# One place per odd step for VectorE jobs, and a second only beside a TensorE job

## The chip, the cores and the metric

The kernel runs on one core of a Trainium2 chip. The metric is device time in microseconds (us), from launch to end. The kernel before takes 6031.49 us in the median of three runs (6030.53 to 6031.90).

The engines are called as the profile calls them: PE is TensorE, DVE is VectorE, ACT is ScalarE, POOL is GpSimd, SP is SyncE, which here only issues DMAs. PEld is the weight load of PE.

## The reference

The input x has 4 images of 128 channels and 64 x 64 pixels, float32. Two layers follow each other:

```
layer 0   Q, K, V = x Wq + bq, x Wk + bk, x Wv + bv      4 heads of 32 channels, 4096 tokens per image
          y = softmax(Q K^T * 32^-0.5) V Wo + bo + x      then a layer norm over channels
layer 1   spatial  = 3x3 convolution of y
          spectral = irfft2( W [Re rfft2(y); Im rfft2(y)] )
          mamba    = in_proj -> causal conv of 4 taps -> silu -> x_proj -> dt = softplus(dt_proj)
                     h_t = exp(dt A) h_(t-1) + dt B_t x_t,   y_t = C_t h_t + D x_t
                     (256 inner channels, 16 states each, 4096 tokens in order)
                     -> times silu(z) -> out_proj
          output   = spatial + spectral + mamba
```

Everything is float32. The attention scores and the scan over 4096 tokens with 16 states are the bulk of the work.

## The kernel before

**Tiles and steps.** An image is cut into 8 chunks of 512 tokens, so there are 32 chunks (`CHUNKS`), and a chunk has two halves with two heads each (64 halves, `HALVES`). The main loop (line 1064) counts steps `t`. A half takes 32 steps, one per block of 128 keys; a chunk takes 64 steps (`SLOT`). Below, "period c" is steps 64c to 64c + 63, and "step s of a period" is t mod 64.

**What every step does, in the order of writing.** `scores_for_exp` (line 488): six matmuls, at line 496, write scores less the row maximum into a PSUM buffer `s2`, and ACT takes the exponential (line 504). `scores_for_max` (line 443): four matmuls, at line 456, write the scores of a half that comes later into a PSUM buffer `s1`, and DVE reduces them to maxima (line 463). There is one buffer `s1` and one `s2`: the next step's matmuls wait until DVE and ACT have read them. `times_values` (line 507): the exponentials of the step before are multiplied with V (line 516) into a buffer `o`; at the end of a half ACT and DVE copy it out (lines 526 and 527).

**The scan.** It runs 144 steps (`LAG`) behind its chunk's attention, one state of one half of the channels in two steps. An even step runs `scan_state` (line 836): a scan on DVE (846), then on POOL a copy of the last column (855), a multiplication with C (856) and a sum (875). An odd step runs `scan_decay` (823), an exponential on ACT (829) into one PSUM buffer, and `scan_input_term` (831), a multiplication on POOL (834) for the state that DVE scans three steps later. There are two buffers each for these terms (`db`) and for the states (`hs`).

**The jobs.** All else is written as jobs (generators). They are put on the list with `plan.at` (lines 1032 to 1059) for a step and with a rank. A job runs until its next `yield`, which says what it needs to go on: `"P"` a place on TensorE, `"D"` on VectorE, `"A"` on ScalarE, `"B"` a free one of two PSUM banks. `Plan.step` (line 125) goes through the jobs once in a step, by rank, then by time, and lets go on each one for which there are places. Places are given anew in each step (lines 1095 to 1106):

```
        elif odd:
            plan.step(t, {"D": 2, "P": 2, "A": 2})
        else:
            plan.step(t, {"D": 0, "P": 0, "A": 1})
```

After step 2048, when the attention is done, there are more places (line 1099), and before the first half too (line 1102).

**Jobs that the text speaks of**, by chunk, with the lines of their parts:
- `project_kv` (342), `project_q` (408): projections; a matmul, then ACT and DVE split the result in two (lines 356, 357 and 418, 419).
- `output_projection` (569): a matmul (575), a sum on DVE (578), four transposes (582), nine DVE instructions for mean and variance (589 to 595), small instructions on ACT and POOL, and the normalisation on DVE (612).
- `normalise` (531): DMAs and a multiplication on POOL (560).
- `mamba_input` (646): transposes (663), then it puts `scan_input` and `spectral` on the list.
- `scan_input` (685), once per half of the channels: a matmul (689), ACT (693 to 695), four taps on DVE with a place each (699, 704), a sigmoid (624; ACT 628, 630, 633, 638 and DVE 636), and a multiplication on POOL (714).
- `scan_bc` (720): two matmuls (726), ACT and DVE (731 to 733).
- `scan_dt` (740), once per half of the channels: a matmul (744), six steps on ACT (750 to 765), then with one place on DVE and ACT an addition on DVE (766) and three multiplications or subtractions on POOL (767 to 769), here called a burst; some steps later ACT scales a tile (776).
- `gate` (779): a matmul (785), ACT, a sigmoid, and a multiplication on POOL (793), for each half of the channels.
- `convolve` (919): ten matmuls (930, 935), then ACT (940).
- `scan_output` (963), `spectral` (889), `flips` (1009).

**Order on an engine.** Nothing reorders what is written: each engine takes its instructions in the order in which the program wrote them (`manual_schedule`, line 181), and waits where its operand or its buffer isn't ready. A job's turn in a step so sets its place in the queues of all engines that it uses, of SP too.

Of the kernel before, what the change touches and what calls it, by code (L numbers as in the profile page):

```python
# [17 lines left out]
P = 128  # L18
# [83 lines left out]
class Plan:  # L102
# [19 lines left out]
    def release(self, bank, steps=1):  # L122
        self.freed.append((self.t + steps, bank))

    def step(self, t, places):

        self.t = t
        self.places |= places
        self.free += [bank for when, bank in self.freed if when <= t]
        self.freed = [e for e in self.freed if e[0] > t]  # L130
        for e in sorted((e for e in self.later if e[0] <= t), key=lambda e: e[:3]):
            self.jobs.append((e[1], e[0], e[2], Job(e[3])))
            self.later.remove(e)
        self.jobs = sorted((j for j in self.jobs if not j[3].done), key=lambda j: j[:3])
        kept = 0
        for *_, job in self.jobs:
            bank = None
            if "B" in job.need and len(self.free) <= kept:
                continue
            if any(c != "B" and not self.places[c] for c in job.need):  # L140
                kept += "B" in job.need
                continue
            for c in job.need:
                if c == "B":
                    bank = self.free.pop(0)
                else:
                    self.places[c] -= 1
            job.advance(bank)

            while not job.done and job.need in ("PAD" if self.late else "P"):  # L150
                if not job.need or not self.places[job.need]:
                    break
                self.places[job.need] -= 1
                job.advance(None)
        self.jobs = [j for j in self.jobs if not j[3].done]
# [6 lines left out]
def attention_then_conv_mamba(  # L162
# [43 lines left out]
    for h in range(HEADS):  # L206
        k, j = divmod(h, 2)
        c = COL["bk"] + k
# [8 lines left out]
    for h in range(HEADS):  # L217
        k, j = divmod(h, 2)
        c = COL["bq"] + h
# [108 lines left out]
    plan = Plan(2, {"x": 2, "f": 1})  # L328
# [114 lines left out]
    def scores_for_max(H, s):  # L443


        k = H % PAIRS
        m, t = divmod(s, TPC)
        assert have["K", k, m] == H // PAIRS // NCH
        if s == 0:
            part[H] = att.tile([P, 2, TPC, NCH], F32, tag="part", name=f"part_{H}")  # L450

        tag = "s2" if H == 0 and s % 2 else "s1"
        sc = psum.tile([P, 2, L], F32, tag=tag, name=f"s1_{H}_{s}")
        for n in range(2):
            for j in range(2):
                nc.tensor.matmul(  # L456
                    sc[:, j, :],
                    QT[H][rows[j], n, t::TPC],
                    KK[k][m][rows[j], :],
                    start=n == 0,  # L460
                    stop=n == 1,
                )
        nc.vector.tensor_reduce(part[H][:, :, t, m], sc, AX.X, ALU.max)  # L463
# [24 lines left out]
    def scores_for_exp(H, m):  # L488

        k = H % PAIRS  # L490
        i, t = divmod(m, TPC)
        assert have["K", k, i] == H // PAIRS // NCH
        s = psum.tile([P, 2, L], F32, tag="s2", name=f"s2_{H}_{m}")
        for n, mov in enumerate((QT[H][:, 0, :], QT[H][:, 1, :], MX[H])):
            for j in range(2):
                nc.tensor.matmul(  # L496
                    s[:, j, :],
                    sel[rows[j], :] if n == 2 else KK[k][i][rows[j], t * P : (t + 1) * P],
                    mov[rows[j], :],
                    start=n == 0,  # L500
                    stop=n == 2,
                )
        e = att.tile([P, 2, L], F32, tag="e", name=f"e_{H}_{m}", bufs=3)
        nc.scalar.activation(e, s, AF.Exp)  # L504
        es[H, m] = e

    def times_values(H, m):

        k = H % PAIRS
        i, t = divmod(m, TPC)  # L510
        assert have["V", i] == H // PAIRS // NCH
        if m == 0:
            po[H] = psum.tile([P, L], F32, tag="o", name=f"po_{H}")
        e = es.pop((H, m))
        for j in range(2):
            nc.tensor.matmul(  # L516
                po[H][used[j], :],
                VA[i][:, t, 2 * k + j, :],
                e[:, j, :],
                start=m == 0,  # L520
                stop=m == NT - 1,
            )
        if m == NT - 1:
            p = po.pop(H)
            oz[H] = att.tile([P, L], F32, tag="oz", name=f"oz_{H}", bufs=1)
            nc.scalar.activation(oz[H][used[0], :], p[used[0], :], AF.Identity)
            nc.vector.tensor_copy(oz[H][used[1], :], p[used[1], :])  # L527
# [295 lines left out]
    def scan_decay(c, v):  # L823
        n, hf = divmod(v, NH)
        k = hf * NS + n

        tag = "o" if plan.t >= HALVES * NT + 2 and v % 2 else "dA"
        dA[c, v] = psum.tile([P, L], F32, tag=tag, name=f"dA_{c}_{k}")
        nc.scalar.activation(dA[c, v], dts[c][hf], AF.Exp, scale=negA[:, k : k + 1])  # L829
# [6 lines left out]
    def scan_state(c, v):  # L836

        n, hf = divmod(v, NH)
        k = hf * NS + n
        assert (c, hf) in scaled  # L840
        late = plan.t > HALVES * NT + 1
        if late:
            hs = flat(VA[v % 4])
        else:
            hs = loc.tile([P, L], F32, tag="hs", name=f"hs_{c}_{k}")
        nc.vector.tensor_tensor_scan(  # L846
            hs,
            dA.pop((c, v)),
            db.pop((c, v)),
            state[:, k : k + 1] if c % NCH else zero,  # L850
            ALU.mult,
            ALU.add,
        )
        if c % NCH < NCH - 1:
            nc.gpsimd.tensor_copy(state[:, k : k + 1], hs[:, L - 1 :])  # L855
        nc.gpsimd.tensor_tensor(hs, hs, bcs[c, n][1], ALU.mult)  # L856
        if hf == NH - 1 and (c, n) in taken:
            spare.append((plan.t + 6, taken.pop((c, n))))
        elif hf == NH - 1:
            ring[0] += 1  # L860
        if late:

            if c not in sums_late:
                sums_late[c] = psum.tile(
                    [P, NH, L], F32, tag=f"s{1 + c % 2}", name=f"acc_{c}"
                )
            terms = [hs] if n else [xss[c][hf], hs]
            for x in terms:
                waiting.append((plan.t + 4, c, hf, x, n == NS - 1 and x is hs))
        elif n == 0:  # L870
            acc = loc.tile([P, L], F32, tag=f"acc{hf}", name=f"acc_{c}_{hf}")
            accs[c, hf] = acc
            nc.gpsimd.tensor_tensor(acc, xss[c][hf], hs, ALU.add)
        else:
            nc.gpsimd.tensor_tensor(accs[c, hf], accs[c, hf], hs, ALU.add)  # L875
# [185 lines left out]
    t = 6 - SLOT  # L1061
    loaded = 0
    end = (CHUNKS + 3) * SLOT
    while t < end or not plan.idle():
        H, m = divmod(t, NT)
        if 0 <= H < HALVES:
            scores_for_exp(H, m)
        h1, s1 = divmod(t + LEAD, NT)
        if 0 <= h1 + 1 < HALVES:
            scores_for_max(h1 + 1, s1)  # L1070
        H, m = divmod(t - 1, NT)
        last = m == NT - 1
        if last and 0 <= H < HALVES:
            times_values(H, m)
        c, s = divmod(t - LAG, SLOT)
        odd = s % 2 == 1
        if -1 <= c < CHUNKS:
            v = c * STATES + s // 2
            if not odd:
                if v >= 0:  # L1080
                    scan_state(*divmod(v, STATES))
            else:
                if 0 <= v + 1 < CHUNKS * STATES:
                    scan_decay(*divmod(v + 1, STATES))
                if 0 <= v + 2 < CHUNKS * STATES:
                    late = t > HALVES * NT
                    scan_input_term(
                        *divmod(v + 2, STATES), nc.vector if late else nc.gpsimd
                    )

                if loaded < CHUNKS * NS and loaded // NS in bcds:
                    if ring[0] or spare and spare[0][0] <= t:
                        scan_load(*divmod(loaded, NS))
                        loaded += 1
        plan.late = t > HALVES * NT
        if plan.late:
            add_states()
            if odd:
                plan.step(t, {"D": 4, "P": 4, "A": 6})
            plan.t = t  # L1100
        elif t < -LEAD:
            plan.step(t, {"D": 4, "P": 4, "A": 4})
        elif odd:
            plan.step(t, {"D": 2, "P": 2, "A": 2})
        else:
            plan.step(t, {"D": 0, "P": 0, "A": 1})
        if not last and 0 <= H < HALVES:
            times_values(H, m)
        t += 1
# [76 lines left out]
```

## Time and profile before

| what | value |
|---|---|
| runs (median of three) | 6031.49 us |
| the profiled execution | 6027.62 us |
| its span, first to last instruction | 6025.8 us |
| mean granted TensorE clock | 0.988 |
| start of step 0 to start of step 2047 | 5676.7 us (128.6 to 5805.3), 2.773 us a step |
| PE busy | 97% of the span |
| POOL, DVE, ACT busy | 74%, 71%, 59% |
| reduction of a step's scores, DVE line 463 | 1221 ns, 2048 times |
| scan, DVE line 846 | 1275 ns |
| exponential of a step's scores, ACT line 504 | 1023 ns, 2048 times |
| exponential for the scan, ACT line 829 | 686 ns, 1024 times |
| term, state and sum, POOL lines 834, 856 and 875 | 1284, 1278 and 1281 ns |

Busy time says little here for PE, as its matmuls overlap and their ends are modelled. It is of more use to look at steps: the time from the first matmul of line 496 in one step to that of the next. A step with no job on PE takes 2.355 us. Rows of the timeline begin with the start and the length in us, then engine, line, operation, output <- inputs, sizes, how many, and in brackets the idle time of the engine just before and what ended it.

### The profile page before, as it was taken

What the parts mean: (1) busy time and instruction counts of PE and PEld (TensorE: products, weight loads), DVE (VectorE), ACT (ScalarE), POOL (GpSimd) and SP (SyncE); (2) the same over time, 40 slices, a digit from 0 to 9 for tenths busy, and PEclk for the clock granted to TensorE, in tenths of its full rate; (3) what the DMA queues carried; (4) which work ended last, traced back from release to release, by engine and by line L of the source; (5) the groups of instructions that cost most, each with busy time, mean ns of one, the idle gap of its engine ahead of it and who ended that gap; (6) DMA issues with size and microseconds to landing.
All of it is one profiled execution on the core that took longest, in us unless ns stands there. A gap on an engine that the chain in (4) does not pass through costs nothing. (4 is left out here: it accounts for less than half of the span.)

```text
span 6025.8 us, 82754 instructions
## 1 busy us (share of the span) xinstructions
PE 5844.9 (97%) x31126; PEld 2786.9 (46%) x31126; DVE 4307.5 (71%) x4505; ACT 3548.3 (59%) x4762; POOL 4486.9 (74%) x4523
## 2 busy tenths in 40 slices
PE   5999999999999999999999999999999999999976
PEld 3444444444444444444444444444444444444422
DVE  4557777777777777777777777777777777777657
ACT  1455666666666666666666666666666666656653
POOL 0006888778888777888787888877888888788887
PEclk7999999999999999999999999999999999999988
DMA  4012222223232222223433322322433222222232
GB/s 125 25 37 56 67 72 75 71 71 111 82 89 73 74 70 74 74 67 88 105 83 82 78 64 73 75 71 68 109 81 86 70 64 64 67 71 64 62 99 90
DMA packets 312722, 456.34 MB, mean 76 GB/s; under 512 B 92768, under 2 KB 94336, under 8 KB 312320
## 3 DMA queue, kind: packets, MB, share of 16 engines
q1 hardware_dynamic: 307664, 449.18, 27.8%
q8 instruction: 244, 4.00, 0.3%
q10 hardware_dynamic: 4656, 1.87, 0.1%
q14 instruction: 158, 1.29, 0.1%
HBM read 376.21 MB, written 66.32 MB: 73 GB/s over the span
## 5 line engine op out<-in xcount | busy, mean ns | idle before, releaser
L463 DVE TENSOR_REDUCE part<-s 128x2 f32<-128x1024 f32 x2048 | 2499.3, 1221 | 1455.6 <-PE s L456 1455.2
L504 ACT ACTIVATE e<-s 128x1024 f32<-128x1024 f32 x2048 | 2095.1, 1023 | 2188.2 <-PE s L496 2178.9
L516 PE MATMUL po<-e,V 128*33 128x512 f32 x8192 | 2180.9, 605 | 2.3 <-DVE oz L527 0.3
L496 PE MATMUL s<-Q,K 64*128 64x512 f32 x8192 | 1504.1, 445 | 7.8 <-ACT e L504 4.3
L496 PEld LDWEIGHTS s<-Q,K 64*128 64x128 f32 x8192 | 610.4, 185 | 1727.4 <-ACT e L504 1253.2
L456 PE MATMUL s<-K,Q 64*128 64x512 f32 x8192 | 1338.7, 404 | 37.9 <-DVE part L463 33.9
L856 POOL TENSOR_TENSOR hs<-hs,bc 128x512 f32<-128x512 f32 x948 | 1211.7, 1278 | 171.0 <-DVE hs L846 102.4
L834 POOL TENSOR_TENSOR db<-u,bc 128x512 f32<-128x512 f32 x948 | 1217.1, 1284 | 0.0
L456 PEld LDWEIGHTS s<-K,Q 64*128 64x128 f32 x8192 | 1122.5, 308 | 191.9 <-DVE part L463 98.9
L875 POOL TENSOR_TENSOR acc<-acc,hs 128x512 f32<-128x512 f32 x894 | 1145.5, 1281 | 70.1
L846 DVE TENSOR_TENSOR_SCAN hs<-dA,state,db 128x512 f32<-128x512 f32 x826 | 1053.1, 1275 | 43.6 <-ACT dA L829 41.9
L496 PE MATMUL s<-MX,sel 64*128 64x512 f32 x4096 | 820.9, 396 | 0.0
L829 ACT ACTIVATE dA<-dt,negA 128x512 f32<-128x512 f32 x1024 | 702.6, 686 | 111.4 <-DVE V L846 69.2
L855 POOL COPY state<-hs 128x1 f32<-128x1 f32 x858 | 160.2, 187 | 775.5 <-DVE hs L846 774.9
L516 PEld LDWEIGHTS po<-e,V 128*33 128x33 f32 x8192 | 305.3, 109 | 733.0 <-issue 694.5
L496 PEld LDWEIGHTS s<-MX,sel 64*128 64x128 f32 x4096 | 384.3, 185 | 92.2 <-DMA MX<-md 0.4
L930 PE MATMUL pf<-xp,cw 128*128 128x512 f32 x576 | 288.8, 620 | 0.0
L560 POOL TENSOR_TENSOR op<-op,rz 128x512 f32<-128x512 f32 x32 | 41.6, 1301 | 184.0 <-DMA rz<-rd 177.3
L846 DVE TENSOR_TENSOR_SCAN hs<-dA,zero,db 128x512 f32<-128x512 f32 x128 | 163.2, 1275 | 0.3
L882 PE MATMUL acc<-V,cst 128*128 128x512 f32 x140 | 91.1, 751 | 65.5 <-POOL V L856 65.2
L930 PEld LDWEIGHTS pf<-xp,cw 128*128 128x128 f32 x576 | 96.7, 188 | 104.9 <-issue 104.1
L714 POOL TENSOR_TENSOR xs<-xs,sg_x 128x512 f32<-128x512 f32 x64 | 82.0, 1281 | 75.1 <-ACT sg_x L638 75.1
(143 smaller groups left out, 3405.8 us busy)
## 6 DMA issues: line engine op xcount, KB each, us to landing
bc<-bcd SPq DMA_DIRECT2D x487, 512.0 KB
Q<-qd SPq DMA_DIRECT2D x256, 128.0 KB
K<-kd SPq DMA_DIRECT2D x64, 256.0 KB
K<-bcd SPq DMA_DIRECT2D x42, 256.0 KB
vd<-vst SPq DMA_DIRECT2D x32, 264.0 KB
V<-vd SPq DMA_DIRECT2D x32, 264.0 KB
xq<-in_x SPq DMA_DIRECT2D x32, 256.0 KB
xk<-in_x SPq DMA_DIRECT2D x32, 256.0 KB
```

What stands on the lines that cost most here:

```text
L456: nc.tensor.matmul(sc[:, j, :], QT[H][rows[j], n, t::TPC], KK[k][m][rows[j], :], start=n == 0, stop=n == 1,)
L463: nc.vector.tensor_reduce(part[H][:, :, t, m], sc, AX.X, ALU.max)
L496: nc.tensor.matmul(s[:, j, :], sel[rows[j], :] if n == 2 else KK[k][i][rows[j], t * P : (t + 1) * P], mov[rows[j], :], start=n == 0, stop= ...
L504: nc.scalar.activation(e, s, AF.Exp)
L516: nc.tensor.matmul(po[H][used[j], :], VA[i][:, t, 2 * k + j, :], e[:, j, :], start=m == 0, stop=m == NT - 1,)
L829: nc.scalar.activation(dA[c, v], dts[c][hf], AF.Exp, scale=negA[:, k : k + 1])
L834: engine.tensor_tensor(db[c, v], us[c][hf], bcs[c, n][0], ALU.mult)
L846: nc.vector.tensor_tensor_scan(hs, dA.pop((c, v)), db.pop((c, v)), state[:, k : k + 1] if c % NCH else zero, ALU.mult, ALU.add,)
L855: nc.gpsimd.tensor_copy(state[:, k : k + 1], hs[:, L - 1 :])
L856: nc.gpsimd.tensor_tensor(hs, hs, bcs[c, n][1], ALU.mult)
L875: nc.gpsimd.tensor_tensor(accs[c, hf], accs[c, hf], hs, ALU.add)
L930: nc.tensor.matmul(pf, cw[:, k, :], xps[c][:, dy : dy + RPC, dx : dx + W], start=k == 0, stop=False)
```

## The change

In an odd step of the main part, jobs get one place on DVE where they got two. Whenever a job takes a place on PE in the upper part of `Plan.step`, one more place on DVE is added, once in a step. Even steps and the steps after the attention keep their numbers. No instruction is added or removed; jobs go on in other steps.

```diff
-    def step(self, t, places):
+    def step(self, t, places, more=False):
+
 
         self.t = t
+        self.more = more
         self.places |= places
...
                 else:
                     self.places[c] -= 1
+                    self.places["D"] += (c == "P") * self.more
+                    self.more &= c != "P"
             job.advance(bank)
...
         elif odd:
-            plan.step(t, {"D": 2, "P": 2, "A": 2})
+            plan.step(t, {"D": 1, "P": 2, "A": 2}, more=True)
```

## The prediction

> **What bounds the kernel now.** I read the page's busy times first, then the windows of start, steps and tail, then the timeline of single steps.
>
> ```profile
> PE 5844.9 (97%) x31126; PEld 2786.9 (46%) x31126; DVE 4307.5 (71%) x4505; ACT 3548.3 (59%) x4762; POOL 4486.9 (74%) x4523
> ```
> ```profile
> core 0: us, PE busy (x) PEld busy (x) DVE busy (x) ACT busy (x) POOL busy (x), PEclk, DMA share, GB/s
> 128.60:5805.30 5676.70, 5643.56 (x30634) 2701.47 (x30630) 4084.29 (x4259) 3450.79 (x4604) 4314.10 (x4348) 1.00 0.28 73
> 0.00:128.60 128.60, 63.17 (x240) 37.32 (x242) 52.49 (x59) 12.25 (x19) 5.05 (x22) 0.76 0.47 147
> 5805.30:6025.80 220.50, 138.22 (x258) 48.07 (x258) 170.70 (x187) 85.23 (x139) 167.75 (x154) 0.82 0.33 101
> ```
>
> PE sets the pace: in the steps it is busy for 5643.6 of 5676.7 us. I laid the jobs of each step, by the order of writing, beside the step's length from the timeline. An empty step takes 2.355 us; one fp32 matmul of a job with 512 columns adds 1.055, a second of its kind in the same step only 0.86. So 5676 = 2047 x 2.355 (4820.7) + 803.4 for the jobs' matmuls + 51 in which PE waits (61 in 190 late steps, -10 elsewhere). These waits are all that DVE, ACT and POOL can cost today, and they repeat at the same steps of each period. The largest, 0.86 us in step 34 of 29 periods:
>
> ```profile
> 2509.43 1.23 DVE L463 TENSOR_REDUCE part<-s 128x2 f32<-128x1024 f32 x1 [1.46 <-PE s L456]
> ...
> 2511.04 0.69 DVE L527 COPY oz<-po 33x512 f32<-33x512 f32 x1 [0.39 <-ACT oz L526]
> ...
> 2511.77 1.28 DVE L846 TENSOR_TENSOR_SCAN hs<-dA,state,db 128x512 f32<-128x512 f32 x1
> ...
> 2512.97 1.20 DVE L463 TENSOR_REDUCE part<-s 128x2 f32<-128x1024 f32 x1
> ...
> 2514.08 0.75 DVE L704 SCALAR_TENSOR_TENSOR conv<-xi,vec,conv 128x512 f32<-128x512 f32 x1
> ...
> 2514.22 0.86 PE L456 MATMUL s<-K,Q 64*128 64x512 f32 x4 [0.47 <-DVE part L463]
> ...
> 2514.74 0.81 DVE L699 TENSOR_SCALAR conv<-xi,vec 128x512 f32<-128x512 f32 x1
> ...
> 2515.46 1.22 DVE L463 TENSOR_REDUCE part<-s 128x2 f32<-128x1024 f32 x1
> ```
>
> Two jobs (704, 699) stand in that odd step, but the reduction that PE waits for is ahead of them: it is late because the end of the half put the copy `oz` and the scan before it. The two jobs only delay the next reduction (2515.46), which costs 0.15 us one step later.
>
> Waits on ACT look like this: after the step's exponential come the scan's and two jobs, the next one starts 0.36 us late, and PE starts 0.15 late at 3803.01.
>
> ```profile
> 3800.15 0.69 ACT L829 ACTIVATE dA<-dt,negA 128x512 f32<-128x512 f32 x1
> ...
> 3800.76 0.68 ACT L356 ACTIVATE khi<-pk,bk 128x512 fp32r<-128x512 f32 x1
> ...
> 3801.33 0.69 ACT L633 ACTIVATE ln_x<-sg_x,ones 128x512 f32<-128x512 f32 x1
> ...
> 3801.95 1.02 ACT L504 ACTIVATE e<-s 128x1024 f32<-128x1024 f32 x1
> ...
> 3803.01 0.50 PE L496 MATMUL s<-Q,K 64*128 64x512 f32 x2
> ```
>
> And a burst of scan_dt on POOL, and what follows:
>
> ```profile
> 3686.99 1.29 POOL L767 TENSOR_TENSOR spe<-u,spe 128x512 f32<-128x512 f32 x1
> 3688.36 1.29 POOL L768 TENSOR_TENSOR dt<-dt,spe 128x512 f32<-128x512 f32 x1
> 3689.73 1.29 POOL L769 TENSOR_TENSOR u<-dt,xs 128x512 f32<-128x512 f32 x1
> 3690.96 0.19 POOL L855 COPY state<-hs 128x1 f32<-128x1 f32 x1
> ...
> 3695.02 0.19 POOL L855 COPY state<-hs 128x1 f32<-128x1 f32 x1
> ...
> 3699.13 0.20 POOL L855 COPY state<-hs 128x1 f32<-128x1 f32 x1
> ```
>
> The burst takes 3.95 us (3686.99 to 3690.96); a state then takes POOL 4.11 (3695.02 to 3699.13), and a pair of empty steps lasts 4.71. So POOL wins back 0.60 a pair, plus what jobs' matmuls add to it.
>
> **The change part by part.** The written order of the changed program shows that in steps 0 to 2047 no odd step carries two DVE jobs: the extra place goes unused, as no second job stands ready behind one that takes PE. So it is "one place". Before, 124 odd steps without a PE job carried two (62 pairs of taps, 31 of a tap and the other half's first, 29 of normalisation and output, two others). Taps spread over steps 33 to 49 of a period, where they filled 31 to 39, and all behind them moves: scan_bc by 9 steps, scan_dt's bursts from steps 61 and 1 to 11 and 13 in 20 periods, half the gates by up to 28.
>
> *DVE.* The 0.15 (29 times) and 0.045 (29 times, step 37) go: -5.7. One 0.86 in step 2 of period 3 goes, as a PE job now stands ahead of it. The 29 waits of 0.86 in step 34 stay, and so do those after the variance job, one place alone (0.43 in step 21). Sum -6.5, between 0 and -10.
>
> *PE.* Matmuls stay, but meet others in their step (counts before to after, added time each): two convolve or convolve's last two 118 to 68 at 1.92: -95.8; scan_input alone 60 to 2 at 1.055, two together 1 to 30 at 1.92: -5.4; gate beside mamba_input 29 to 0 at 1.93, mamba_input alone 2 to 31 at 0.99, gate alone 30 to 52 at 1.055: -4.0; convolve's last alone 0 to 23: +24.3; both scan_dt 30 to 8 at 0.655, scan_dt beside convolve 2 to 45 at 1.48: +49.4; scan_bc alone 30 to 1 at 1.73, scan_bc ahead of convolve 0 to 30: +37.4; small ones +9.5. Together +15.4. The last price is from a single step with scan_bc ahead of another matmul (5.28 us, 2.92 added); taken as 1.73 + 0.86 the sum is +5.5. I take 15.4, because the order in the step is the same, and keep 5.5.
>
> *ACT.* Odd steps without a PE job but with two ACT jobs cost as shown. New are step 9 (query projection and scan_dt, 20 times, about 0.17), step 11 (two scan_dt, 22 times, 0.12), step 53 (logarithm and spectral, 23 times, 0.10, as the 0.115 of a like pair) and some 19 others of 0.1: +10.3. Gone are steps 45 (23 x 0.15), 41 (31 x 0.035) and 8 of 0.115: -5.4. Sum +4.9, between 0 and +11.
>
> *POOL.* Before, the bursts stand four steps apart with convolve's matmuls (1.92) around them, and POOL is at most 2.7 us late. Now they stand two apart, just ahead of the chunk's first states. The term (834) written in step t ends 3.94 us before the scan of step t + 3 wants it, plus the matmuls between. Step 13's burst leaves 2 x 3.95 - 2 x 0.60 - 0.13 - 1.06 (the matmul of step 13) = 5.5 late; there are 3.94 + 1.06 (gate, step 15) + 0.59 (transposes, 17) = 5.6. So 18 periods just make it. The two with flips on POOL between (periods 9 and 17, 1.55 more) miss by 1.5 each. Periods 3 and 4 (bursts at 9 and 11) miss by 1.4 and 0.35. Periods 25, 27, 29 and 31 (bursts at 5 and 9, then a gate's 1.29 and line 560's 1.29) miss by 4, 1.6, 1.6 and 2.7; periods 26, 28 and 30 by 0.3. That is 15.5; DVE has some 0.3 in hand before PE waits, so +13. Scan, reduction and PE's matmuls queue behind such a late term. Bounds: 0 (POOL hides them as it does now) to +30 (the 18 miss by nearly 1 us as well).
>
> *Tail and start.* Period 32 takes a burst that ran before step 2048, and one gate: 3.95 + 1.29 on POOL, 1.06 on PE, into 40 us in which POOL is busy for 34. Between 0 and +9; I take 4. The start has no job held back.
>
> In the tail, line 856 writes and reads at 1500 ns in the group of V and K tiles against 1278 in the steps. The Trainium skill ("SBUF — State Buffer", section "Who interferes with whom") says that a DVE instruction with two SBUF inputs shuts out a GpSimd instruction that reads SBUF; there DVE makes the scan's terms from two such inputs, so the rule speaks against work moved into the tail. By it the burst there would take 3 x 0.22 = 0.7 us more, an estimate, and the sum 31.5 in place of 30.8.
>
> SP's loads of B and C are written by when their three buffers come free, in step 7 of a period; scan_bc's write is now in step 0, 7 steps (over 16 us) ahead, so I cost them at nothing. If that cover went, POOL would wait for them in step 13.
>
> Sum: -6.5 + 15.4 + 4.9 + 13 + 4 = +30.8 on the profiled execution's 6027.6: 6058.4. The median of the runs shown is 3.9 above it: 6062.
>
> **The rivals.** About 0.2% (12 us) is what a measurement of this kernel can tell from no change.
>
> *The step 34 wait belongs to the two DVE jobs.* Then 29 x 0.86 = 25 us go as well, and the sum is +5.9: 6037, no change. It decides from 0.65 us a period on. For it: it is the step right after the pair. Against it: the order of the rows above.
>
> *POOL hides both bursts everywhere and scan_bc costs 0.33 less.* -6.5 + 5.5 + 4.9 + 0 + 4 = +8: 6039, the same. For it: no wait for POOL is among DVE's today.
>
> *POOL misses in all periods.* +30 in place of 13: 6079. For it: the margin in 18 periods is 0.1 us of 5.6, and a late scan passes straight into the variance job's wait in step 21.
>
> *The second place is used after all*, so that the delays shrink: the order written excludes it.
>
> **How the numbers follow.** The forecast of slower work holds 0.80 together, of which the forecast itself 0.60 and POOL everywhere 0.20; step 34 has 0.07 and POOL hidden 0.13. Of these I give 0.13 to within 0.2% (6019 to 6044) and 0.07 to faster, since all gains together, -10, would need every cost at its lower end. The range takes in the low cases from 6037 and the high one with the tail's upper end, 6084.
>
> **What would show it.** In the profile after: 0.86 us before line 456 in step 34 still, but not the 0.15 in step 35; steps with scan_bc of 5.28 us; POOL without a gap from step 12 to beyond 20; DVE's scan waiting for `db` in steps 14 to 18 of periods 25 to 31. I am wrong if POOL takes the bursts without a late scan, or if a wait appears at the taps' new places.

## The result and the profile after

The changed kernel takes 6197.97 us in the median (four runs, 6193.25 to 6200.10), the kernel before 6031.69 beside it. The ratio is 1.0275, with a 95% interval from 1.0263 to 1.0287: slower by 166 us. The forecast of 6062 had the direction, and a fifth of the size. Line numbers of the changed kernel are 4 higher than before from line 154 on.

The busy times on the page, and the windows of steps, start and tail (columns as in the prediction):

```profile
PE 5890.3 (95%) x31126; PEld 2798.8 (45%) x31126; DVE 4338.0 (70%) x4505; ACT 3542.4 (57%) x4762; POOL 4482.3 (72%) x4523
```
```profile
core 0: us, PE busy (x) PEld busy (x) DVE busy (x) ACT busy (x) POOL busy (x), PEclk, DMA share, GB/s
129.60:5965.30 5835.70, 5690.17 (x30636) 2715.29 (x30632) 4113.68 (x4256) 3437.39 (x4592) 4305.39 (x4344) 0.99 0.27 71
0.00:129.60 129.60, 62.71 (x240) 35.84 (x242) 52.48 (x59) 12.26 (x19) 5.04 (x22) 0.80 0.48 145
5965.30:6191.50 226.20, 137.46 (x256) 47.65 (x256) 171.84 (x190) 92.70 (x152) 171.87 (x158) 0.82 0.33 98
```

Of the 165.7 us between the two spans (6191.5 and 6025.8), the steps have 159.0 (5835.7 against 5676.7), the tail 5.7 and the start 1.0. In the steps, every engine is busy for a smaller share of their time than before: none became the bound, and PE waits. Laying the jobs of each step beside its length once more gives 804.9 us for the jobs' matmuls (804.7 before) and 210.1 us in which PE waits (51.3 before). The split between the two is good to some 3 us, as the median length of like steps stands for the length without a wait. By step of the period:

| where PE waits | before, us | after, us |
|---|---|---|
| steps 25 and 26 | below 1 | 112.0 |
| step 32 | below 1 | 38.0 |
| steps 16, 18 and 20 | below 1 each | 15.0 |
| step 34 | 25.0 | 22.0 |
| step 21 | 12.3 | 8.1 |
| steps 35 and 37 | 5.2 | below 1 each |

Two waits that the prediction doesn't mention, at 25 and 32, make 150 of the 166 us. The table of waits names both (engine and line, what it waited for, us together, times, longest). It counts an engine's idle time just before an instruction, which is less than what the steps lose:

```profile
ACT zg L795 <- POOL acc L985: 108.1, 24, 4.9
...
PE s L500 <- ACT e L508: 87.5, 43, 3.8
...
PE s L500 <- DMA MX<-md: 28.4, 5, 6.7
```

**Steps 24 to 26 of a period**, from the timeline of period 12:

```profile
2356.68 1.28 POOL L797 TENSOR_TENSOR zg<-zg,sg_z 128x512 f32<-128x512 f32 x1
...
2357.91 1.26 POOL L838 TENSOR_TENSOR db<-u,bc 128x512 f32<-128x512 f32 x1
...
2359.13 2.49 POOL L985 TENSOR_TENSOR acc<-acc,zg 128x512 f32<-128x512 f32 x2
2360.43 0.60 ACT L795 ACTIVATE zg<-pz 128x512 f32<-128x512 f32 x1 [4.92 <-POOL acc L985]
2360.92 1.02 ACT L508 ACTIVATE e<-s 128x1024 f32<-128x1024 f32 x1
...
2361.99 1.22 PE L500 MATMUL s<-Q,K 64*128 64x512 f32 x4 [3.79 <-ACT e L508]
```

`zg` has one buffer for each half of the channels. ACT's copy into it (795) belongs to the gate of chunk 10; POOL's product (985), which reads the values of chunk 9 from the same buffer, begins at 2359.13. The copy can't start before the first of the two products ends, at 2360.4. The exponential of the step's scores is written behind it on ACT, and so is 3.8 us late for PE.

How did they come so close? Before, the product is written in step 18 and the copy in step 29, eleven steps later. In the same period of the kernel before, POOL is done with the buffers 23 us ahead of the copy, which waits for nothing:

```profile
2295.92 2.55 POOL L981 TENSOR_TENSOR acc<-acc,zg 128x512 f32<-128x512 f32 x2
...
2321.83 0.59 ACT L791 ACTIVATE zg<-pz 128x512 f32<-128x512 f32 x1
```

After, the second gate of chunk 9 is among the jobs that moved from the period before: it runs in steps 15 to 22. `scan_output` waits for it (`while not all(gates[c])`), so the products are written in step 23. The gate of chunk 10 moves forward in turn, from 27 to 23, as the matmuls of `scan_output` no longer stand there, and its copy is written in step 24. One step lies between them, and POOL runs the products 5.7 us after step 24 has begun (2353.41 by the step's first matmul). The written order has this in 24 periods, and the table of waits counts 24 such waits.

**Step 32**, where a half begins, in period 25:

```profile
4772.98 0.21 DVE L473 TENSOR_REDUCE mx<-part 128x8 f32<-128x64 f32 x1
...
4773.65 0.33 SPq L479 DMA_DIRECT2D md<-neg  x1
...
4778.61 1.28 POOL L860 TENSOR_TENSOR hs<-hs,bc 128x512 f32<-128x512 f32 x1 [2.61 <-DVE hs L850]
...
4779.92 0.37 SPq L816 DMA_DIRECT2D bc<-bcd  x1
...
4780.40 2.44 SPq L485 DMA_DIRECT2D MX<-md  x4
...
4785.23 1.09 PE L500 MATMUL s<-MX,sel 64*128 64x512 f32 x2 [5.16 <-DMA MX<-md]
```

The job `maxima` gathers the row maxima of the coming half (DVE), stores them (479) and loads them again as rows (485). It needs a place on DVE, and with one place it gets it in step 29, as `output_projection` and `scan_output` take those of 25 and 27; before, it shared step 27. The four loads are issued at 4780.40, after step 32 has begun (4779.34), and are on the chip 4.8 us later. In this row SP also held them until POOL had read a `bc` buffer (4778.61 + 1.28 = 4779.89), because a load of `bc` is written ahead of them. In the same period of the kernel before, where step 32 begins at 4659.94, the loads are issued 5.95 us ahead of it:

```profile
4649.08 0.33 SPq L475 DMA_DIRECT2D md<-neg  x1
4653.99 2.44 SPq L481 DMA_DIRECT2D MX<-md  x4
```

There 4.9 us lie between store and loads, and 6.75 after, so some 1.8 us of the lateness are the hold, an estimate from these rows; the rest is the later place. Five periods have it (3, 25, 27, 29, 31), at 7.3 to 7.9 us each.

**Step 34 of period 12**, the rows that answer those of the prediction:

```profile
2386.50 0.69 DVE L531 COPY oz<-po 33x512 f32<-33x512 f32 x1 [0.38 <-ACT oz L530]
...
2387.22 1.28 DVE L850 TENSOR_TENSOR_SCAN hs<-dA,state,db 128x512 f32<-128x512 f32 x1
...
2388.42 1.20 DVE L467 TENSOR_REDUCE part<-s 128x2 f32<-128x1024 f32 x1
...
2389.54 0.81 DVE L703 TENSOR_SCALAR conv<-xi,vec 128x512 f32<-128x512 f32 x1
...
2389.68 0.86 PE L460 MATMUL s<-K,Q 64*128 64x512 f32 x4 [0.47 <-DVE part L467]
...
2390.58 1.23 DVE L467 TENSOR_REDUCE part<-s 128x2 f32<-128x1024 f32 x1 [0.23 <-PE s L460]
```

One tap stands there in place of two, PE waits 0.47 at line 460 as before, and the next reduction is on time: the small wait of step 35 is gone.

**The bursts on POOL**, the second one of period 12 and the term that it delays:

```profile
2332.46 1.30 POOL L771 TENSOR_TENSOR spe<-u,spe 128x512 f32<-128x512 f32 x1
...
2336.43 0.19 POOL L859 COPY state<-hs 128x1 f32<-128x1 f32 x1
...
2339.30 1.27 POOL L838 TENSOR_TENSOR db<-u,bc 128x512 f32<-128x512 f32 x1
...
2340.63 1.27 DVE L850 TENSOR_TENSOR_SCAN hs<-dA,state,db 128x512 f32<-128x512 f32 x1
```

The term ends at 2340.57, and the scan that wants it starts at 2340.63 without a wait. The prediction had a margin of 0.1 us here.

### The profile page after: what moved, and what is told of

It reads as the page before. It is cut to its first block, busy times and chain, and to the rows that moved or that the text cites. A ratio compares the mean times of both kernels' runs of the same rounds, so it can differ in the third digit from the quotient of the medians.

```text
span 6191.5 us, 82690 instructions
## 1 busy us (share of the span) xinstructions
PE 5890.3 (95%) x31126; PEld 2798.8 (45%) x31126; DVE 4338.0 (70%) x4505; ACT 3542.4 (57%) x4762; POOL 4482.3 (72%) x4523
```

## The experiments

**The gate's buffer.** The changed kernel, with a second buffer (`zh0`) beside that of the first half of the channels (`zg0`), used in every other chunk.

```diff
-            z = loc.tile([P, L], F32, tag=f"zg{hf}", name=f"zg_{c}_{hf}", bufs=1)
+            z = loc.tile([P, L], F32, tag="zh0" if hf == 0 and c % 2 else f"zg{hf}", name=f"zg_{c}_{hf}", bufs=1)
```

> The changed kernel with a second tile for the gate of the first half of the channels (odd chunks use the new tile), and no other edit; the written order of jobs is the same. Theory (one tile is the wait): the copy of the gate's input on ACT no longer waits for POOL's product of the chunk before, the 3.9 us in step 25 and 1.4 us in step 26 of some 20 periods go (82.8 + 29.3 us), and the time falls from 6198 to about 6086. Rival (POOL's lateness is the cause, and the tile only where it shows): POOL is as late as before, the wait moves to the next user of POOL's results, and the time stays above 6150.

Measured: 6080.31 us (6074.48 to 6083.29), ratio 1.0078 (1.0063 to 1.0093). PE's waits fall from 210.1 to 92.4 us; those of steps 25 and 26 are gone, step 32 keeps 38.7. The written order is the same, so the reuse of one buffer costs 118 us (6197.97 less 6080.31), 71% of the change's loss.

**The row maxima.** The changed kernel, with `maxima` ranked ahead of the other jobs.

```diff
-        plan.at(H * NT - LEAD, 0, maxima(H))
+        plan.at(H * NT - LEAD, -1, maxima(H))
```

> The changed kernel with the job of the row maxima ahead of all others in rank, so that it has its place in step 25 of the period always. Theory (the maxima come too late for their DMA round trip): the wait of PE for the row of maxima in step 32 of five periods (7.3 to 7.9 us each, 38 together) goes, and the time falls to about 6160; the jobs that give way move by two steps. Rival (that wait is a DMA queue's, whatever the step of issue): 6198 within 0.2%.

Measured: 6153.39 us (6146.41 to 6158.88), ratio 1.0200 (1.0185 to 1.0215). Step 32's wait is gone, 25 and 26 keep 75.5 and 27.7. So the edit is worth 45 us by the medians. That is a little more than the 38 us of step 32, because steps 25 and 26 lose 9 us of their 112 as well: other jobs move too when `maxima` goes first.

**Both mended together**, the two edits in one kernel.

> The second gate tile and the maxima first together. Theory (the two waits add up and explain all that the forecast lacked): 6198 - 112 - 38 = 6048, some 16 us over the kernel before, near what the forecast's own terms give without them. Rival (they overlap, or POOL's lateness shows in new places): above 6090.

Measured: 6057.16 us (6055.53 to 6059.15), ratio 1.0041 (1.0027 to 1.0055). With the two waits away, 25.6 us of loss remain, where the terms of the forecast came to 30.8. They aren't the same terms, though. Against the kernel before, this profile has 16.1 us more of waits (67.4), 4.1 more of jobs' matmuls (808.8), and 2.4 and 8.9 more in start and tail. The largest new wait, 12.0 us in step 27, points to its cause in the trace: it stands in periods 4 to 24 alone, mostly 0.57 us, and in these periods alone `maxima`'s second negation (line 476, which is 472 in the kernel before; in the first of a period's two jobs) takes 1.17 to 1.20 us where its median is 0.17. `variance_split` below shows the same wait at its full size.

**The gate held back.** Does the closeness of copy and product do it, or the buffer's being single in itself? Here the gate of a chunk waits until four steps after the products of the chunk before.

```diff
+        while c and done.get(c - 1, end) + 4 > plan.t:
+            yield ""
...
+        done[c] = plan.t
```

> The changed kernel in which the gate of a chunk may start only four steps after POOL was given the product of the chunk before with its gate (one tile, no second one). Theory (the wait is the reuse of the one gate tile, one step after its reader was written): the 112 us in steps 25 and 26 go as with a second tile, the wait for the row of maxima (38 us) stays: about 6085. Rival (POOL's lateness stops ACT wherever the gate stands): above 6150.

Measured: 6103.89 us (6103.35 to 6108.91), ratio 1.0121 (1.0106 to 1.0137). The waits of steps 25 and 26 are gone with one buffer too. A new one of 40.9 us stands in step 18, 1.76 in most periods. Its rows in period 12:

```profile
2307.42 1.28 DVE L853 TENSOR_TENSOR_SCAN hs<-dA,state,db 128x512 f32<-128x512 f32 x1 [1.03 <-POOL db L841]
...
2310.19 1.27 POOL L799 TENSOR_TENSOR zg<-zg,sg_z 128x512 f32<-128x512 f32 x1
...
2311.42 1.27 POOL L841 TENSOR_TENSOR db<-u,bc 128x512 f32<-128x512 f32 x1
...
2312.72 1.28 DVE L853 TENSOR_TENSOR_SCAN hs<-dA,state,db 128x512 f32<-128x512 f32 x1 [0.72 <-POOL db L841]
```

The bursts themselves stand two steps earlier here, at 9 and 11, and the other gate's product (799) comes on POOL behind them; the scan waits for its term twice. The first of the two late terms stands ahead of the product (2307.42, against 2310.19), so the bursts' place alone makes it late; the prediction had periods with bursts at 9 and 11 miss, too. Only the second can be the product's doing. How the two share the 1.76 us was not run apart.

**Who owns step 34?** Now the kernel before, with no place for DVE jobs in step 33. This is the first rival of the prediction.

```diff
-            plan.step(t, {"D": 2, "P": 2, "A": 2})
+            plan.step(t, {"D": 0 if t % SLOT == 33 else 2, "P": 2, "A": 2})
```

> The kernel before with no place on DVE in step 33 of a period, so that the two tap jobs that stand there move to step 35. Theory (the 0.86 us that PE waits in step 34 come from the copy at the end of the half and the scan ahead of the reduction): the wait stays in 29 periods, and the time is 6031 within 8 us. Rival (the two jobs in the odd step cause it): 25 us go, 6007 or less.

Measured: 6038.99 us (6036.30 to 6042.16), ratio 1.0012 (1.0002 to 1.0021). Step 34 waits 24.9 us, as before. Its rows, with no job on DVE at all:

```profile
2341.18 0.69 DVE L527 COPY oz<-po 33x512 f32<-33x512 f32 x1 [0.38 <-DMA bc<-bcd]
...
2341.90 1.28 DVE L846 TENSOR_TENSOR_SCAN hs<-dA,state,db 128x512 f32<-128x512 f32 x1
...
2343.10 1.20 DVE L463 TENSOR_REDUCE part<-s 128x2 f32<-128x1024 f32 x1
...
2344.36 0.86 PE L456 MATMUL s<-K,Q 64*128 64x512 f32 x4 [0.47 <-DVE part L463]
```

The rival falls: what is left ahead of the late reduction is the copy and the scan. But the kernel got slower by 7 us, with waits in steps 9 and 47 (9.0 and 10.9 us, some 0.4 and 0.5 in 21 and 22 periods). Two steps ahead of each, in 7 and 45, two DVE jobs now meet in an odd step without a PE job. So the situation that the change aims at does cost something there. It costs next to nothing in steps 35, 37 and 39, where this kernel has such pairs in 31 periods each; what makes the difference was not tested.

**A PE job in step 33.** If DVE can't catch up at the end of a half, PE's own work can give it the time: no place on PE in step 31, so that its job goes to 33.

```diff
-            plan.step(t, {"D": 2, "P": 2, "A": 2})
+            plan.step(t, {"D": 2, "P": 0 if t % SLOT == 31 else 2, "A": 2})
```

> The kernel before with no place on TensorE in step 31 of a period, so that the second half's input projection (1.06 us) moves to step 33, and with it one tap. Theory (the reduction of step 33 is late by the copy and the scan; a job's matmul in step 33 keeps PE busy meanwhile): the 0.86 us of step 34 go in 29 periods, and most of the 0.15 in step 35: about 6003. Rival (the moved taps make as many new waits, as without a job in step 33): 6020 or more.

Measured: 6006.19 us (6005.95 to 6008.53), ratio 0.9957 (0.9945 to 0.9970). Step 34's wait is gone; PE waits 18.5 us in all, 12.6 of it in step 21. This kernel beats both.

**The variance job in two.** The kernel before, with a place on DVE each for its statistics and its sums, and one place on PE in step 31.

```diff
+        yield "D"
         for t in range(TPC):
             nc.vector.bn_aggr(mv[:, t, :], st[:, t, :])
...
+            plan.step(t, {"D": 2, "P": 1 if t % SLOT == 31 else 2, "A": 2})
```

> The kernel before with the variance job's nine instructions on DVE split over two steps (a place more, after the four statistics), which moves what follows by two steps, and one place on TensorE in step 31, so that one input projection stands in 33. Theory: the 0.43 us in step 21 (12 us) and the 0.86 in step 34 (25 us) go; the taps then stand as in the run without a job in step 33 and bring that run's 20 us of new waits in steps 9 and 47 (two DVE jobs with no TensorE job): about 6010. Rival (the new waits don't come, as the projection's job has moved too): 5995 or less.

Measured: 6040.24 us (6031.36 to 6049.17), ratio 1.0012 (1.0004 to 1.0021): a miss by 30 us. Steps 21 and 34 are free of waits, and steps 9 and 47 have the expected ones (8.7 and 11.0), but step 27 has a new one of 50.8, about 1.7 in most periods. Its rows:

```profile
2320.39 1.28 POOL L876 TENSOR_TENSOR acc<-acc,hs 128x512 f32<-128x512 f32 x1
...
2320.62 1.08 DVE L471 TENSOR_SCALAR neg<-mx 128x8 fp32r<-128x8 f32 x1
...
2321.63 1.29 POOL L835 TENSOR_TENSOR db<-u,bc 128x512 f32<-128x512 f32 x1
2321.73 1.21 DVE L472 SCALAR_TENSOR_TENSOR neg<-mx,neg 128x8 fp32r<-128x8 f32 x1
...
2322.86 1.21 DVE L463 TENSOR_REDUCE part<-s 128x2 f32<-128x1024 f32 x1
...
2324.13 0.86 PE L456 MATMUL s<-K,Q 64*128 64x512 f32 x4 [1.30 <-DVE part L463]
```

Two instructions over 8 elements a partition take 1.08 and 1.21 us, where the shortest of their lines take 0.17. The section on hardware takes this up.

**The same, with one place on DVE in steps 7 and 45**, so that the pairs of steps 9 and 47 go.

```diff
+            plan.step(t, {"D": 1 if t % SLOT in (7, 45) else 2, "P": 1 if t % SLOT == 31 else 2, "A": 2})
```

> As the split variance job, with one place on DVE in steps 7 and 45 of a period, where two DVE jobs would stand without a TensorE job. Theory (two DVE jobs without a TensorE job cost some 0.4 us each time, and one place there removes it): 20 us less than with two places, about 5990. Rival (what is held back there moves scan_bc, the bursts and the gates, as the change does, and costs more than the 20 us): 6010 or more.

Measured: 6001.41 us (6001.13 to 6002.97), ratio 0.9949 (0.9936 to 0.9963). The value lies between the two expectations: step 27 keeps 16.7 us, and all other steps together come to 1.4. The 39 us under `variance_split` aren't the theory's 20 alone. The waits of steps 9 and 47 go, 20 us; step 27 loses 34, as `maxima`'s first negation is stretched over 0.8 us in ten of the periods 0 to 30 only, the ten in which step 27 still waits (10, 11, 18, 19 and 25 to 30); and the jobs' matmuls cost some 15 more, because `scan_bc` and `scan_dt` now stand beside `convolve`. So one place where a pair costs something did what was expected of it, and the rest came by the way; one place everywhere costs 166 us.

**One addition, on ACT.** As `tensor_job_in_33`, with the addition of line 595 done by ACT.

```diff
+    eps = const.tile([P, 1], F32, name="eps")
+    nc.vector.memset(eps, LN_EPS)
...
-        nc.vector.tensor_scalar(v, mv[:, :, 1], LN_EPS, None, ALU.add)
         yield ""
+        nc.scalar.activation(v, mv[:, :, 1], AF.Identity, bias=eps)
```

> The kernel before with no place on TensorE in step 31, as in tensor_job_in_33, and with the addition of line 595 (v = variance + eps) moved from DVE to ACT, one step later, ahead of the logarithm. In tensor_job_in_33 this addition over 128x4 takes 724 ns in the median on DVE beside POOL's work, 171 at the least, and PE waits 0.43 us in step 21 of 29 periods behind the variance job (12.6 us together). If these 0.7 us are what makes the reduction late there, the wait goes whole: about 5994 us against 6006, ratio 0.9935. Rival: the eight instructions before it are long enough alone, or the work that takes the addition's place beside POOL is stretched instead: step 21 keeps its 0.43 and the time stays at 6003 to 6008, or rises by up to 6 if ACT's extra 0.2 us a period shows in PE's wait for the exponential.

Measured: 5990.01 us (5987.12 to 5992.78), ratio 0.9929 (0.9916 to 0.9943). The 12.6 us of step 21 are gone, and PE's waits come to 1.7 in all. The timeline of step 20 and 21 with the addition on DVE:

```profile
2288.05 1.28 POOL L873 TENSOR_TENSOR acc<-xs,hs 128x512 f32<-128x512 f32 x1
...
2288.62 0.72 DVE L595 TENSOR_SCALAR v<-mv 128x4 f32<-128x4 f32 x1
2289.26 1.21 DVE L463 TENSOR_REDUCE part<-s 128x2 f32<-128x1024 f32 x1
...
2290.53 0.86 PE L456 MATMUL s<-K,Q 64*128 64x512 f32 x4
```

and with the addition on ACT:

```profile
2281.15 0.28 DVE L593 BATCH_NORM_AGGREGATE mv<-st 128x2 f32<-128x6 f32 x3
...
2281.49 1.23 DVE L465 TENSOR_REDUCE part<-s 128x2 f32<-128x1024 f32 x1
2281.99 0.29 ACT L598 ACTIVATE v<-mv,eps 128x4 f32<-128x4 f32 x1
...
2283.16 0.64 PE L458 MATMUL s<-K,Q 64*128 64x512 f32 x4
```

The reduction now follows the sums at once. This is the fastest of the kernels, 41 us under the one before.

## Why the prediction was wrong

The step that failed is the half sentence "and all behind them moves: scan_bc by 9 steps, scan_dt's bursts from steps 61 and 1 to 11 and 13 in 20 periods, half the gates by up to 28". The bursts, `scan_bc` and the gates were then costed as work on PE and POOL; the reuse of the gates' buffers, and the wait of `scan_output` for a late gate, stand in the sum at nothing, without a reason. For each moved job the load that it puts on an engine was counted; it wasn't asked which buffer it writes, who reads that last, and which job waits for it to end. The second gate, whose matmul comes 26 steps late in most periods and whose product 16 (step 22 where it was 6), holds `scan_output` for five steps, and the products there then collide with the next chunk's copy: 112 us in the trace, 118 by the second buffer. The closing sentence did allow for a wait "at the taps' new places", but the wait came ahead of those places, at other jobs. (By the written order `scan_bc` moves by 10 steps in most periods, not 9.)

`maxima` wasn't in the working at all. "They filled 31 to 39" counts the taps; that other jobs with places on DVE now form a row through steps 25, 27 and 29 follows from the same rule. It has a due time, with a store and a load behind it: 38 us in the trace; the experiment that mends it gains 45, with 9 of them in steps 25 and 26.

The other steps, against the profile after:

- *DVE, −6.5, between 0 and −10.* Steps 35 and 37 lose their 5.2 us, as said (5.7). Step 34 stays at 22.0, as said, and the experiment with no job in step 33 shows why. Steps 2, 21, 33 and 34 change by −1.0, −4.2, +2.9 and −3.0: together −10.5, just outside the bounds. Step 21's wait was to stay at 0.43; it is about 0.2 in most periods.
- *PE, +15.4 or +5.5.* Measured +0.2. The 5.28 us for scan_bc ahead of another matmul, from one step, is right: 5.27 in 30 steps. The term that was mis-sized is "mamba_input alone 2 to 31 at 0.99": it takes 0.585 in 31 steps, so 29 × 0.405 = 11.7 less. Only two steps before have it alone, and the price fits one of them (3.35 us; the other took 4.63). The trace before had a better one: the four transposes of `output_projection`, of the same shape, stand alone in 31 steps there and cost 0.586. `spectral` alone at 3.44 for 3.53 has 2.5 more.
- *ACT, +4.9.* Steps 10 and 12 have 3.0 and 2.3 us, at 0.1 us each; steps 42, 46 and 48 lost 5.5. About nothing came of the sum.
- *POOL, +13, between 0 and +30.* Measured 15.0 in steps 16, 18 and 20, and in the periods that were named: 1.19 in 9 and in 17, 0.94 in 27 and in 29, 1.82 in 31, 0.01 in the eighteen that "just make it" (by its own rows a burst takes 3.97 us, not 3.95, so their margin was nearer 0.05 than 0.1).
- *Tail +4, start 0.* Measured +5.7 and +1.0. The tail has twelve instructions of bursts now. The six of the first two bursts take 8.26 us against 6 × 1.28 = 7.68: 0.1 us more for each, where the prediction's estimate had 0.22.

The measured terms make −10.5 + 0.2 − 0.1 + 15.0 + 5.7 + 1.0 = 11.3, the two waits 150, and step 27 has another 5.2: together 166.5, for 165.7 in the spans.

Of the rivals, step 34 as the two jobs' own is shown false. POOL missing in all periods didn't happen here, though `gate_held` shows that bursts two steps earlier, with a gate's product behind them, bring it about in most. That the extra place goes unused stands: the written order is the same without it, which is no measurement but leaves nothing to measure. What stays open is why the tail of `both_mended` is 8.9 us longer; nothing was run for it. The 2.4 us of its start lie within what the start takes in the profiles of all these kernels, 128.2 to 132.1 us.

## What to carry to other kernels

When a scheduling rule delays jobs, list for every delayed job its buffers with the last reader and the next writer, and the jobs that wait for its end, before adding up engine time: a single buffer that was reused eleven steps later cost 118 us here once it was reused one step later. Look next for jobs with a due time and a DMA round trip behind them, and move those by rank, not by chance. And limit a resource only in the steps whose waits show it: one place in two of the 32 odd steps took away the 20 us of waits that they were meant for (39 us in all, 6040.24 to 6001.41); one place in all of them added 166.

## What the runs showed of the hardware

A small DVE instruction can take as long as the POOL instruction beside it. The addition of line 595 (4 elements a partition) takes over 0.6 us in 27 of 32 cases before, where its shortest is 0.17. Each of the 27 ends within 0.03 us of the end of a POOL instruction, as in the rows above: 2288.62 + 0.72 = 2289.34, and POOL's ends at 2288.05 + 1.28 = 2289.33. The negations of lines 471 and 472 go the same way: 1 and 8 of 64 take over 0.6 us before, 29 and 31 of 64 in `variance_split`, up to 1.2 us, all with their ends within 0.03 us of one of POOL's. In both traces no short case of these three instructions (under 0.4 us) lies wholly inside a POOL instruction. The maximum's reduction, 64 elements a partition, takes 0.20 to 0.22 us in all 64 cases before, and 59 of them lie wholly inside a POOL instruction.

This agrees with the Trainium skill ("SBUF — State Buffer", section "Who interferes with whom"): `tensor_scalar` in its two-port modes, and DVE instructions with two SBUF inputs where the GpSimd instruction reads SBUF, contend with GpSimd for a pair of ports and block fully until it is free, while `tensor_reduce` never does. No run here looks at the ports themselves. The price where PE waits for what DVE does next is measured: moving one addition of 4 elements from DVE to ACT took 16 us off this kernel.
